# Preparing the weights at the start of a transformer kernel: biases by layout, order of the first loads, and TensorE and ScalarE in place of GpSimd

## The chip, the cores and the metric

The kernel runs on one core of a Trainium2 chip. The metric is the device time of one execution in microseconds (us). A core has five engines that each work through a queue of instructions of their own, in order: PE (TensorE, matmuls, with its weight loads), DVE (VectorE), ACT (ScalarE), POOL (GpSimd) and SP (SyncE, which here issues DMA transfers). They wait for each other by semaphores.

## What is computed

An input x of 8 sequences of 512 tokens with 256 features goes through four residual blocks: attention A, a gated feed-forward network (FFN), causal attention B, and the same FFN again.

```
x = x + attention_a(layernorm(x))
x = x + ffn(layernorm(x))
x = x + attention_b(layernorm(x))
x = x + ffn(layernorm(x))

# attention_a: 16 heads of 64; the 64 channels of one token attend to each other, causally
Q, K, V = (x @ Wq + bq) / 8, x @ Wk + bk, x @ Wv + bv        # 256 -> 1024 each
w = softmax(where(mask, -inf, Q[..., :, None] * K[..., None, :]))
out = (w @ V) @ Wo + bo
# attention_b: 16 heads of 16 over 512 tokens, causal, W_attn (256 -> 768), W_proj, biases
# ffn: silu(x W1 s1) * (x W2 s2), then gelu(. H1 h1), gelu(. H2 h2), then (. W3) s3
```

## The kernel before

Nearly all the time goes into attention A's outer products, which exist for each token and head and have no sum over a contraction that PE could do. The class `AttentionA` cuts them into steps. A tile is 128 tokens (index `i`, four to a sequence `b`) and a group of four heads (`g`, four groups); it has four units (`u`) of squares of the causal triangle, so a tile takes four steps, and the list `todo` runs over b, g, i, u. In step `n` the unit n is multiplied out (`scores`, lines 771 and 784: units 0 and 2 on POOL, 1 and 3 on DVE), unit n-1 gets its exponential on ACT (`exps`, 793 and 798), unit n-2 is weighted by V on DVE (`weigh`, 805 and 808) and, but for the smallest unit, halved by an accumulating DMA that POOL issues (`halve`, 814). Later steps fold (POOL, 819), reduce (DVE, 845) and add up the rows (POOL, 852). The projections of a tile on PE (`project`, 741 for K and 746 for Q and V) stand three steps ahead of its first unit, its normalised x eight steps ahead (`normed`, `turned_over`, 542 and 548), with the moments ten ahead (`measure`, lines 524 to 532).

The order of instructions on PE, DVE, ACT and POOL is the order in which the program writes them. Each step is written in three parts; after each part the main loop may write a piece of two other generators: `later_weights`, the preparation of weights, and `after_a`, the FFN and attention B of the sequence that has left attention A. SP's order is set by a scheduler. Blocks of SBUF of 8 KB a partition come from a pool of seven (`block`), so a late holder delays a load that wants its place.

Weights must be prepared because the normalised x carries a constant 1 in its last feature instead of the feature itself: a layer norm's features add up to zero, so that x's last feature is minus the sum of the others. The last row of a weight is therefore subtracted from every other row, and its place is taken by the bias. The steps of the beginning are, by line:

- `load_x(0)` (307) loads the first sequence, then `last_qv` and `last_k` (323, 324) are loaded as the last rows of Wq, Wv and Wk for all groups, copied to 128 partitions; then the weights of the four groups (335, 336).
- `fit_qkv(g)` subtracts the last row (344, 346; on DVE for group 0, on POOL for the others), lets SP put the bias into the last row (347, 348) and write the result to DRAM (349, 350). Group 0 is fitted before everything, groups 1 to 3 in steps 0 to 2. From then on `load_w` reads a group's weights from DRAM (624, 626).
- `later_weights` (from step 2, one piece after each part, so three a step) makes three bf16 parts of two biases with ACT, POOL and DVE (421 to 432), multiplies w3 by its scale (POOL, 451), fits attention B's weights (POOL, 456) and writes them to DRAM (460 to 462).
- It ends with `bound_scores`, which squares the weights on ACT (373, 374) after loading them again (368, 370), sums the squares in 96 small matmuls with a result of one column (382), and takes a square root (388) and maxima (389 to 402): a bound on the scores, for a flag that chooses a slower path, at the end.
- `bias_row` (468) adds a bias to a result on PE: ones in three rows times the three bf16 parts.

Of the kernel before, what the change touches and what calls it, by code (L numbers as in the profile page):

```python
# [9 lines left out]
F32 = mybir.dt.float32  # L10
F32R = mybir.dt.float32r
BF16 = mybir.dt.bfloat16
# [272 lines left out]
def fast_path(ctx: ExitStack, tc: tile.TileContext, k, t, flag):  # L285
# [24 lines left out]
    def block(name, dtype=F32):  # L310

        return hp.tile([P, HB], dtype, tag="h", name=name)

    x_first = load_x(0)

    wqv_r, wk_r = t.wqv.rearrange("(c p) g f -> p c g f", p=P), t.wqkv[1].rearrange("(c p) f -> p c f", p=P)
    wqv_d = dram.tile([NG, P, DC * 2 * GW], F32, name="wqv_d")  # L320
    wk_d = dram.tile([NG, P, DC * GW], F32, name="wk_d")
    last_qv, last_k = block("last_qv"), block("last_k")
    nc.sync.dma_start(last_qv, t.wqv[D - 1 : D].rearrange("o g f -> o (g f)").broadcast_to([P, HB]))
    nc.sync.dma_start(last_k[:, :HID], t.wqkv[1][D - 1 : D].broadcast_to([P, HID]))
    fitted = []
    for g in range(NG):
        if g == 0:

            wqv = wp.tile([P, DC, 2 * GW], F32, tag="wqv", name=f"wqv_0_{g}")
            wk = wp.tile([P, DC, GW], F32, tag="wk", name=f"wk_0_{g}")  # L330
        else:
            both = block(f"fit_{g}")
            wqv = both[:, : DC * 2 * GW].rearrange("p (c f) -> p c f", c=DC)
            wk = both[:, DC * 2 * GW : DC * 3 * GW].rearrange("p (c f) -> p c f", c=DC)
        nc.sync.dma_start(wqv, wqv_r[:, :, g, :])
        nc.sync.dma_start(wk, wk_r[:, :, g * GW : (g + 1) * GW])
        fitted.append((wqv, wk))

    def fit_qkv(g):

        wqv, wk = fitted[g]
        eng = nc.vector if g == 0 else nc.gpsimd
        qv_last = last_qv[:, g * 2 * GW : (g + 1) * 2 * GW].unsqueeze(1).to_broadcast([P, DC, 2 * GW])
        eng.tensor_tensor(wqv, wqv, qv_last, ALU.subtract)
        k_last = last_k[:, g * GW : (g + 1) * GW].unsqueeze(1).to_broadcast([P, DC, GW])
        eng.tensor_tensor(wk, wk, k_last, ALU.subtract)
        nc.sync.dma_start(wqv[P - 1 : P, DC - 1, :], t.b_qv[g : g + 1, :])
        nc.sync.dma_start(wk[P - 1 : P, DC - 1, :], t.b_a[1:2, g * GW : (g + 1) * GW])
        nc.sync.dma_start(wqv_d[g].rearrange("p (c f) -> p c f", c=DC), wqv)
        nc.sync.dma_start(wk_d[g].rearrange("p (c f) -> p c f", c=DC), wk)  # L350
# [8 lines left out]
    def bound_scores():  # L359
# [7 lines left out]
        for c in range(DC):  # L367
            nc.sync.dma_start(sqv[c], wqv_r[:, c])
        sk = block("sk").rearrange("p (c f) -> p c f", c=DC)
        nc.sync.dma_start(sk, wk_r)  # L370
        yield
        for c in range(DC):
            nc.scalar.activation(sqv[c], sqv[c], AF.Square)
            nc.scalar.activation(sk[:, c], sk[:, c], AF.Square)
            yield
# [30 lines left out]
    wbvp_d = dram.tile([P, 2 * DC * D], F32, name="wbvp_d")  # L406
    bias16 = const.tile([P, 2, D], BF16, name="bias16")[0:3]
    ones16 = const.tile([P, P], BF16, name="ones16")
    nc.gpsimd.memset(ones16, 1.0)

    def later_weights():

        braw = block("braw")[0:3].rearrange("p (n f) -> p n f", n=4)
        part16 = block("part16", BF16)[0:3, : 2 * D]
        for j, row in enumerate((t.bo, t.b_bp)):
            nc.sync.dma_start(braw[:, 0, j * D : (j + 1) * D], row.broadcast_to([3, D]))
        yield
        for j in range(3):  # L420
            nc.scalar.copy(part16, braw[:, 0])
            nc.scalar.copy(braw[:, 2], part16)
            nc.gpsimd.tensor_tensor(braw[:, 0], braw[:, 0], braw[:, 2], ALU.subtract)
            yield
            if j == 0:
                nc.vector.tensor_scalar_mul(braw[:, 3], braw[:, 2], ident[0:3, 0:1])
            else:
                nc.vector.scalar_tensor_tensor(
                    braw[:, 3], braw[:, 2], ident[0:3, j : j + 1], braw[:, 3], ALU.mult, ALU.add
                )  # L430
        yield
        nc.scalar.copy(bias16.rearrange("p j f -> p (j f)"), braw[:, 3])

# [7 lines left out]
        nc.sync.dma_start(w3, t.w3.rearrange("(c p) f -> p c f", p=P))  # L441
        nc.sync.dma_start(wbqk, t.w_bqk.rearrange("(c p) j f -> p c (j f)", p=P))
        nc.sync.dma_start(wbvp[:, 0], t.w_bv.rearrange("(c p) f -> p c f", p=P))
        nc.sync.dma_start(wbvp[:, 1], t.w_bp.rearrange("(c p) f -> p c f", p=P))
        nc.sync.dma_start(
            rows[:, :n_qk], t.w_bqk[D - 1 : D].rearrange("o j f -> o (j f)").broadcast_to([P, n_qk])
        )
        nc.sync.dma_start(rows[:, n_qk : n_qk + D], t.w_bv[D - 1 : D].broadcast_to([P, D]))
        yield
        for c in range(MC):  # L450
            nc.gpsimd.tensor_tensor(w3[:, c, :], w3[:, c, :], s3, ALU.mult)
            if c % 2:
                yield
        for w, row, cols in ((wbqk, t.b_bqk_row, slice(0, n_qk)), (wbvp[:, 0], t.b_bv, slice(n_qk, n_qk + D))):
            for c in range(DC):
                nc.gpsimd.tensor_tensor(w[:, c], w[:, c], rows[:, cols], ALU.subtract)
                yield
            nc.sync.dma_start(w[P - 1 : P, DC - 1, :], row)

# [6 lines left out]
    def bias_row(ps, j):  # L466

        nc.tensor.matmul(ps, ones16[0:3, :], bias16[:, j, :], start=False, stop=False)

# [134 lines left out]
    class AttentionA:  # L604
# [33 lines left out]
        def step(self, n):  # L638
# [16 lines left out]
            b, i, g, u = self.at(n + 10)  # L655
            if u == 0 and g == 0 and i == 0:
                self.measure(b)
# [67 lines left out]

        def measure(self, b):
            mv = small.tile([P, NT, 2], F32, tag="mv_a", name="mv", bufs=2)
            rstd = small.tile([P, NT], F32, tag="rstd_a", name="rstd", bufs=2)
            for i in range(NT):
                moments(self.x[b][:, i, :], mv[:, i, :])  # L730
            scales(mv, rstd, means[:, b, 0, :])
            for i in range(NT):
                self.rn[b, i] = rstd[:, i : i + 1], means[:, b, 0, i : i + 1]
# [607 lines left out]
    with tc.manual_schedule(engines={ET.PE, ET.DVE, ET.Activation, ET.Pool}):  # L1341
        a = AttentionA()
        prep = later_weights()
        fit_qkv(0)
        weights = None
        done, spent = after_a(), 0
        for n in range(-10, a.steps):
            for part, _ in enumerate(a.step(n)):
                if n >= 2:
                    next(prep, None)  # L1350
                while 3 * spent * each < total * (3 * (n - each - 11) + part + 1):
                    spent += next(done)
            if 0 <= n < NG - 1:
                fit_qkv(n + 1)
        for _ in done:
# [88 lines left out]
```

## Time and profile before

| | us |
|---|---|
| median of 3 runs | 4007.05 (4005.77 to 4012.08) |
| profiled execution | 4009.55 |
| its span, first to last instruction | 4007.6 |
| accumulating DMA of 1 MB (w<-w), issue to landing, median | 7.7 |
| the same in the first 160 us | 9.9 |
| matmul pass 128x512, L746, mean | 0.715 |
| matmul of the bias, L468, median of 64 | 0.278 |

The profile is taken on one execution. Its page has the busy time of each engine, then the span in 40 equal slices with each engine's busy share in tenths, the granted clock of PE (PEclk, in tenths) and the share of the 16 DMA engines; then the chain of work that ended last, and the costliest groups of instructions by line, each as output<-input. The name of an engine with a q (SPq) is its queue: there stand the issues of DMAs, which are not counted as busy. A float32 matmul is two matmul records in the trace, one for each pass.

### The profile page before, as it was taken

What the parts mean: (1) busy time and instruction counts of PE and PEld (TensorE: products, weight loads), DVE (VectorE), ACT (ScalarE), POOL (GpSimd) and SP (SyncE); (2) the same over time, 40 slices, a digit from 0 to 9 for tenths busy, and PEclk for the clock granted to TensorE, in tenths of its full rate; (3) what the DMA queues carried; (4) which work ended last, traced back from release to release, by engine and by line L of the source; (5) the groups of instructions that cost most, each with busy time, mean ns of one, the idle gap of its engine ahead of it and who ended that gap; (6) DMA issues with size and microseconds to landing.
All of it is one profiled execution on the core that took longest, in us unless ns stands there. A gap on an engine that the chain in (4) does not pass through costs nothing.

```text
span 4007.6 us, 37678 instructions
## 1 busy us (share of the span) xinstructions
PE 2958.0 (74%) x12328; PEld 2012.2 (50%) x12328; DVE 3376.7 (84%) x3777; ACT 2337.2 (58%) x3145; POOL 3098.1 (77%) x3051
## 2 busy tenths in 40 slices
PE   1543478777876888768787788768787778768988
PEld 0311145355653656346553566346653556436847
DVE  4899988998889888998989988998889988897115
ACT  2433465666755766666755767567656667555342
POOL 6688888887888887887888888888888878886211
PEclk7555689888987989889897889879898899879999
DMA  8566777668776777668776688668877687767304
GB/s 240 114 141 145 146 182 182 147 161 199 199 162 126 195 188 196 150 147 210 174 192 139 168 198 214 147 131 198 195 181 151 154 199 205 155 133 210 126 29 167
DMA packets 118653, 671.07 MB, mean 167 GB/s; under 512 B 12704, under 2 KB 31915, under 8 KB 43824
## 3 DMA queue, kind: packets, MB, share of 16 engines
q0 software_dynamic: 78336, 570.46, 62.9%
q1 hardware_dynamic: 40112, 98.11, 6.8%
q8 instruction: 100, 1.64, 0.2%
q14 instruction: 105, 0.86, 0.1%
HBM read 255.90 MB, written 9.96 MB: 66 GB/s over the span
## 4 chain that ended last, share of the span: by engine, by line
DVE 38%; PE 16%; POOL 14%; DMA 12%; issue 8%; ACT 8%; POOLq 0%; DVEq 0%; ACTq 0%
DVE red L845 15%; DMA w<-w 12%; DVE w L808 10%; PE ph L1120 5%; ACT w L798 3%; POOL w L819 3%; DVE ws L808 3%; POOL w L784 3%; PE pqkb L1167 3%; DVE ws L784 3%; POOL acc L852 3%; DVE w L784 2%; POOL w L814 2%; DVE acc L856 2%; POOL h L1036 2%
## 5 line engine op out<-in xcount | busy, mean ns | idle before, releaser
L798 ACT ACTIVATE w<-w 128x2048 f32<-128x2048 f32 x384 | 734.2, 1913 | 653.8 <-POOL w L784 440.8
L1120 PE MATMUL ph<-h,hidden 128*128 128x512 f32 x4096 | 1047.9, 412 | 77.4 <-POOL h L1036 45.5
L784 POOL TENSOR_TENSOR w<-k 128x1024 f32<-128x1024 f32 x512 | 1076.2, 2102 | 9.6 <-ACT k L762 9.0
L1120 PEld LDWEIGHTS ph<-h,hidden 128*128 128x128 f32 x4096 | 795.3, 196 | 282.1 <-POOL h L1036 55.9
L808 DVE TENSOR_TENSOR w<-w,qv 128x1024 f32<-128x1024 f32 x768 | 899.8, 1213 | 22.4 <-ACT w L798 22.3
L845 DVE TENSOR_REDUCE red<-w 128x128 f32<-128x1024 f32 (+1 forms) x384 | 601.8, 1567 | 171.6 <-DMA w<-w 94.6
L819 POOL TENSOR_TENSOR w<-w 128x1024 f32<-128x1024 f32 x256 | 643.1, 2512 | 72.5 <-DMA w<-w 71.9
L814 POOL DMA_DIRECT2D w<-w x384 | 337.1, 878 | 339.7 <-issue 134.8
L852 POOL TENSOR_TENSOR acc<-acc,red 128x256 f32<-128x256 f32 (+1 forms) x640 | 471.0, 736 | 152.3 <-DVE red L845 124.5
L845 DVE TENSOR_REDUCE red<-ws 128x256 f32<-128x2048 f32 (+1 forms) x256 | 435.5, 1743 | 0.0
L746 PE MATMUL qv<-wqv,xnta 128*128 128x512 f32 x512 | 299.3, 715 | 89.9 <-DVE ws L808 82.4
L808 DVE TENSOR_TENSOR ws<-ws,qv 128x1024 f32<-128x1024 f32 (+3 forms) x512 | 294.7, 638 | 49.4 <-ACT ws L798 49.4
L1052 PE MATMUL pw<-xnt,gate 128*128 128x512 f32 (+2 forms) x1152 | 298.8, 419 | 24.9 <-ACT silu L1028 18.0
L784 DVE TENSOR_TENSOR w<-qv,k 128x1024 f32<-128x1024 f32 x256 | 301.3, 1219 | 3.6
L784 DVE TENSOR_TENSOR ws<-qv,k 128x1024 f32<-128x1024 f32 (+3 forms) x512 | 299.8, 648 | 0.0
L868 PE MATMUL bank<-ident,acc 128*128 128x128 f32 x256 | 64.3, 341 | 287.5 <-ACT k L761 287.1
L798 ACT ACTIVATE ws<-ws 128x1920 f32<-128x1920 f32 x128 | 231.5, 1809 | 75.3 <-DVE ws L784 74.7
L1052 PEld LDWEIGHTS pw<-xnt,gate 128*128 128x128 f32 x1152 | 227.6, 213 | 82.1 <-ACT silu L1028 22.3
L1229 ACT ACTIVATE eb<-psb 128x256 f32<-128x256 f32 (+3 forms) x512 | 182.2, 443 | 146.6 <-PE psb L1226 146.3
L1146 PE MATMUL pof<-w,h 128*128 128x256 f32 x1024 | 247.9, 396 | 19.4 <-ACT h L1085 19.4
L1085 ACT ACTIVATE h<-ph,s_sb 128x512 fp32r<-128x512 f32 (+1 forms) x256 | 171.1, 688 | 145.9 <-PE ph L1120 144.6
L856 DVE RECIPROCAL acc<-acc 128x256 f32<-128x256 f32 x128 | 223.2, 1744 | 12.3 <-POOL acc L852 12.3
(143 smaller groups left out, 4723.5 us busy)
## 6 DMA issues: line engine op xcount, KB each, us to landing
w<-w POOLq DMA_DIRECT2D x384, 1024.0 KB, 7.7
hidden<-in_h POOLq DMA_DIRECT2D x128, 1024.0 KB, 7.9
gate<-in_w12p POOLq DMA_DIRECT2D x32, 1024.0 KB, 9.0
w<-w_d SPq DMA_DIRECT2D x16, 1024.0 KB, 12.0
wqv<-wqv_d SPq DMA_DIRECT2D x31, 512.0 KB
wo<-in_wo SPq DMA_DIRECT2D x32, 256.0 KB, 7.4
wbqk<-wbqk_d SPq DMA_DIRECT2D x8, 1024.0 KB
w<-in_h SPq DMA_DIRECT2D x8, 1024.0 KB, 7.0
```

Of the source, the lines that this page charges most:

```text
L746: nc.tensor.matmul(qv.rearrange("p j f -> p (j f)"), xnt[:, c, :], wqv[:, c, :], start=(c == 0), stop=(c == DC - 1),)
L784: eng.tensor_tensor(e, rows(q).to_broadcast(shape), columns(kt[:, 0]).to_broadcast(shape), ALU.mult)
L798: nc.scalar.activation(e, e, AF.Exp, scale=C**-0.5)
L808: nc.vector.tensor_tensor(ev, e, columns(qv[:, 1]).to_broadcast(list(e.shape)), ALU.mult)
L814: nc.gpsimd.dma_start(w[:, :2048], w[:, 2048:], accum_op=ALU.add)
L819: nc.gpsimd.tensor_tensor(w[:, :1024], w[:, :1024], w[:, 1024:2048], ALU.add)
L845: nc.vector.tensor_reduce(red, self.columns_of(w, n, off, nsq), AX.X, ALU.add)
L852: nc.gpsimd.tensor_tensor(rows, rows, part.rearrange("p a (x i) -> p a x i", i=n), ALU.add)
L856: nc.vector.reciprocal(acc[:, 0, :], acc[:, 0, :])
L1052: nc.tensor.matmul(pj[:, toks], w[:, m % 4, j, c, :], xs[:, p, c, toks], start=(p == 0 and c == 0), stop=(p == 1 and c == DC - 1),)
L1120: nc.tensor.matmul(pss[j], w[:, j, c, :], h_in(p, c), start=(p == 0 and c == 0), stop=(p == 1 and c == MC - 1),)
L1146: nc.tensor.matmul(po, h(0, c)[:, i * P : (i + 1) * P], w3[:, c, :], start=(c == 0), stop=False)
```

## The change

The bias now lies in the last row of the weight from the start (arrays `wqvb`, `wkb`, `w_bqkb`, `w_bvb`, laid out before the launch), and the subtraction leaves that row out. The DMAs that put a bias in place are gone. The original rows are still read from `wqv` and `wqkv`.

The first loads are the first tile of x, the weights of group 0 and their last rows for this group alone; the other tiles of x, the other groups and the last rows as single rows follow. `measure` takes a range of tiles: the first tile's moments are taken before group 0 is fitted, those of the other three after it. `fit_first` subtracts in four DVE instructions, two of them over 127 partitions.

The other groups and attention B's weights are fitted by `less_row`: an identity matmul brings a part of the weight to PSUM, a matmul of one row (-1 for every row but the last, times the last row) subtracts from it, and ACT copies the result back one step later. w3 is scaled two chunks at a time. `later_weights` now starts at step 3 and writes one piece a step; it takes in the groups 1 to 3, then w3, attention B and the bounds. The two biases stay float32, one row each, in `rows_of_1`.

```diff
+    x_first = xp.tile([P, NT, D], F32, tag="x", name="x_0")
+    nc.sync.dma_start(x_first[:, 0, :], t.x[0, :P, :])
...
-    last_qv, last_k = block("last_qv"), block("last_k")
-    nc.sync.dma_start(last_qv, t.wqv[D - 1 : D].rearrange("o g f -> o (g f)").broadcast_to([P, HB]))
-    nc.sync.dma_start(last_k[:, :HID], t.wqkv[1][D - 1 : D].broadcast_to([P, HID]))
+    last_first = block("last_first")
...
         nc.sync.dma_start(wqv, wqv_r[:, :, g, :])
         nc.sync.dma_start(wk, wk_r[:, :, g * GW : (g + 1) * GW])
+        if g == 0:
+            row_qv, row_k = last_first[:, : 2 * GW], last_first[:, 2 * GW : 3 * GW]
+            nc.sync.dma_start(row_qv, t.wqv[D - 1 : D, 0].broadcast_to([P, 2 * GW]))
+            nc.sync.dma_start(row_k, t.wqkv[1][D - 1 : D, :GW].broadcast_to([P, GW]))
+            for i in range(1, NT):
+                nc.sync.dma_start(x_first[:, i, :], t.x[0, i * P : (i + 1) * P, :])
...
+    def fit_first():
+
+        wqv, wk = fitted[0]
+        for w, row in ((wqv, row_qv), (wk, row_k)):
+            for c, rows in enumerate((slice(0, P), slice(0, P - 1))):
+                nc.vector.tensor_tensor(w[rows, c], w[rows, c], row[rows], ALU.subtract)
...
+    def less_row(w, c, row, p0):
+
+        ps = ps_f.tile([P, 2 * GW], F32, tag="pf", name="pfit")[:, : w.shape[-1]]
+        nc.tensor.matmul(ps, ident, w, start=True, stop=False)
+        nc.tensor.matmul(ps, from_rows[p0 : p0 + 1, c, :], row, start=False, stop=True)
+        return ps
+
     def fit_qkv(g):
...
-        eng.tensor_tensor(wqv, wqv, qv_last, ALU.subtract)
...
-        eng.tensor_tensor(wk, wk, k_last, ALU.subtract)
-        nc.sync.dma_start(wqv[P - 1 : P, DC - 1, :], t.b_qv[g : g + 1, :])
-        nc.sync.dma_start(wk[P - 1 : P, DC - 1, :], t.b_a[1:2, g * GW : (g + 1) * GW])
...
+        for w, row, p0 in rows:
+            pss = [less_row(w[:, c], c, row, p0) for c in range(DC)]
+            yield
+            for c, ps in enumerate(pss):
+                nc.scalar.copy(w[:, c], ps)
+            yield
...
             nc.scalar.activation(sqv[c], sqv[c], AF.Square)
+            yield
             nc.scalar.activation(sk[:, c], sk[:, c], AF.Square)
...
-        for j in range(3):
-            nc.scalar.copy(part16, braw[:, 0])
-            nc.scalar.copy(braw[:, 2], part16)
-            nc.gpsimd.tensor_tensor(braw[:, 0], braw[:, 0], braw[:, 2], ALU.subtract)
...
+            nc.sync.dma_start(biases[j][:, :D], row)
+        for g in range(1, NG):
+            yield from fit_qkv(g)
...
-        for c in range(MC):
-            nc.gpsimd.tensor_tensor(w3[:, c, :], w3[:, c, :], s3, ALU.mult)
-            if c % 2:
-                yield
...
-                nc.gpsimd.tensor_tensor(w[:, c], w[:, c], rows[:, cols], ALU.subtract)
-                yield
-            nc.sync.dma_start(w[P - 1 : P, DC - 1, :], row)
+        for c in range(0, MC, 2):
+            pair = w3[:, c : c + 2, :]
+            nc.gpsimd.tensor_tensor(pair, pair, s3.unsqueeze(1).to_broadcast(list(pair.shape)), ALU.mult)
+            yield
+        for w, off, width in ((wbqk, 0, 2 * GW), (wbqk, 2 * GW, 2 * GW), (wbvp[:, 0], 0, D)):
+            row = rows[0:1, n_qk if width == D else off :][:, :width]
+            pss = [less_row(w[:, c, off : off + width], c, row, 0) for c in range(DC)]
+            yield
+            for c, ps in enumerate(pss):
+                nc.scalar.copy(w[:, c, off : off + width], ps)
+            yield
...
-        nc.tensor.matmul(ps, ones16[0:3, :], bias16[:, j, :], start=False, stop=False)
+        nc.tensor.matmul(ps, biases[j][:, D:], biases[j][:, :D], start=False, stop=False)
...
-        fit_qkv(0)
+        a.measure(0, range(1))
+        fit_first()
+        a.measure(0, range(1, NT))
...
-                if n >= 2:
+                if n >= 3 and part == 2:
                     next(prep, None)
...
-            if 0 <= n < NG - 1:
-                fit_qkv(n + 1)
```

## The prediction

> **What bounds the kernel now.** I read the page first (busy shares, the 40 slices), then the windows of the beginning, the chain of waits, the list of waits and the timeline of the first 165 us.
>
> ```profile
> PE 2958.0 (74%) x12328; PEld 2012.2 (50%) x12328; DVE 3376.7 (84%) x3777; ACT 2337.2 (58%) x3145; POOL 3098.1 (77%) x3051
> ...
> DVE  4899988998889888998989988998889988897115
> ...
> 27.91:53.21 25.30, 3.98 (x12) 1.93 (x12) 15.01 (x18) 12.96 (x17) 23.79 (x15) 0.68 0.52 140
> 53.21:85.78 32.57, 5.08 (x10) 2.62 (x10) 22.44 (x25) 9.30 (x9) 31.54 (x30) 0.55 0.98 291
> 85.78:141.08 55.30, 26.56 (x115) 22.16 (x115) 26.45 (x32) 16.64 (x15) 23.13 (x20) 0.56 0.57 140
> 141.08:164.87 23.79, 9.83 (x18) 4.38 (x18) 23.76 (x26) 9.64 (x11) 19.98 (x18) 0.57 0.55 112
> 164.87:188.59 23.72, 9.68 (x18) 4.20 (x18) 23.68 (x26) 9.12 (x9) 20.74 (x19) 0.64 0.66 133
> ```
>
> The second line is DVE's busy tenths in slices of 100 us: full until the last tenth, except the first slice. The windows (columns: length, busy us of PE, PE weight load, DVE, ACT, POOL, then clock, DMA share, GB/s) run from one tile's first score (DVE, L771) to the next. From 141 us on, a tile takes 23.72 us with DVE busy for 23.68 of them: DVE sets the pace. The three tiles before took 25.30, 32.57 and 55.30 us, and DVE worked for only 63.9 of those 113.2.
>
> ```profile
> 12.91 1.23 DVE L344 TENSOR_TENSOR wqv<-wqv,last_qv 128x1024 f32<-128x1024 f32 x1 [10.39 <-DMA wqv<-in_wqv]
> ...
> 22.44 2.07 PE L741 MATMUL bank<-wk,xnta 128*128 128x256 f32 x4 [0.46 <-ACT xnta L669]
> ...
> 27.91 0.42 DVE L771 TENSOR_TENSOR acc<-qv,k 128x256 f32<-128x256 f32 x1 [11.03 <-ACT k L762]
> ...
> 31.78 2.35 POOL L344 TENSOR_TENSOR fit<-fit,last_qv 128x1024 f32<-128x1024 f32 x1
> ...
> 87.34 1.40 SPq L370 DMA_DIRECT2D sk<-in_wqkv  x1
> ...
> 107.15 1.06 ACT L374 ACTIVATE sk<-sk 128x1024 f32<-128x1024 f32 x1 [21.88 <-DMA sk<-in_wqkv]
> ...
> 110.86 1.79 ACT L798 ACTIVATE ws<-ws 128x1920 f32<-128x1920 f32 x1
> ...
> 112.68 2.35 DVE L808 TENSOR_TENSOR ws<-ws,qv 128x1024 f32<-128x1024 f32 x4 [24.68 <-ACT ws L798]
> ...
> 141.08 0.41 DVE L771 TENSOR_TENSOR acc<-qv,k 128x256 f32<-128x256 f32 x1
> ```
>
> The timeline (start, us, instruction; in brackets the idle time before it and what ended it) names the losses: DVE waits to 12.91 for weights; the first score comes at 27.91; POOL does weights between scores; and at 85 us ACT stands in its own order before the Square of sk, whose load SP issued only at 87.34. That load costs DVE 24.68 us. Then PE works through the norms (L382, in the chain from 110.06 to 129.82) with the projections of the fourth tile among them.
>
> **What the skill says.** The Trainium skill, "SBUF — State Buffer", section "Who interferes with whom", says a VectorE instruction with two SBUF inputs contends with a GpSimd instruction that reads SBUF. The trace fits: L390, 24 elements a partition, took 1.38 us beside POOL. So weight work taken from POOL also frees DVE a little; I count nothing for it. The same page, "The DMA setup-cost knee", gives about 2 us fixed for a transfer; the x loads of 128 KB here land in 2.0 us (median). "TensorE: Matmul & The Clock Gate", "What's actually happening", says an idle TensorE runs at half clock; PEclk is 0.5 in 100 to 125 us. I price new matmuls at the slow durations. "ScalarE: Activation LUTs", "What ACT_TABLE_LOAD costs", says 1283 ns; the trace has 1.28 us at L388.
>
> **The change part by part.**
>
> First weights. Before, x (0.5 MB), two broadcast blocks (1.5 MB) and wqv (0.5 MB) stood ahead of the first subtraction: 2.5 MB at 153, 303 and 307 GB/s in the first three windows of 4 us. Now one x tile, wqv, wk and two short rows are needed: 0.13 + 0.5 + 0.25 + 0.26 + 0.13 = 1.27 MB, reached at about 6.1 us by those rates; with 2 us of landing, 8.3 us (bounds 7 and 10). Four subtractions 512, 512, 256, 256 wide: 512 took 0.69 on DVE, 256 about 0.42: 2.2 us. Three tiles' moments at 0.53: 1.6. POOL's scales 2.0, ACT xn 0.65, PE transposes 0.7, ACT copy 0.4: the first L741 at about 16.0 instead of 22.44. The first tile's xn is made earlier now, so only one xn is in that chain. From L741 to L771 it stays 5.5 us. First score at 21.6 instead of 27.91: 6.3 us. The two one-row DMAs of the bias into wqv and wk (L347, L348), which SP had issued after DVE, go too.
>
> The first three tiles. POOL loses three pairs of L344 and L346 (3 x 2.35 + 4.4 = 11.5), three L423 (4.3), L456 twice 2.34 and twice 0.96 (6.6). What remains, walked through with the durations above: POOL's first scores 21.6 to 25.4, ACT exp to 27.3, DVE L808 to 29.7, w16 to 32.1, ws to 34.4, second scores back from ACT at 35.0, DVE to 37.4, so the second tile's L771 at 37.8. The next period has stalls of about 2 us for the accumulating DMA (8 us from issue) and ends at 62.5. The third is steady: 86.2. DVE's own work from first to fourth L771 was 63.9 - 2.9 (L426, L428, gone) - 2.8 (norm, moved) = 58.2; my 64.6 is that with 6.4 of stalls. Against 141.08: **54.9 us** less.
>
> What comes after 86 us that was before 141:
> - Three groups' weights on PE and ACT (L365, L366, L380 of the new file). A 128x512 float32 matmul is two passes of 0.94 at half clock (3.75 for four); a wqv part is eight passes, 7.5 us, a wk part 4.2. A period has 9.4 busy on PE: 21.1 of 23.7 with both. They stand behind a projection (done about 6 us after DVE's L808 of ws) and ahead of nothing due within a step; the ACT copies (0.6 + 0.6 for 512 wide, as L1188's 599 ns) come one step of 5.93 us later, ACT being busy 9.1 of 23.7 and idle about 3 before each exp. I take 0; without the cover 9 copies times 2 us = 18.
> - SP: the write-backs wait for ACT, and the reload of group 1 (L643) stands behind one of them (L382 of group 2). That copy is done a step earlier than PE frees wqv, so 0.
> - w3 (L469): four POOL products 512 wide, L346's 1.27 to 1.71 each, 5.6 us in one period in which POOL waits 2.7 for DVE (before L814). Cost 0 to 5.6: I take 3.
> - Norms: DVE about 2.8, ACT 2 x 1.28 + 0.19 for the table. The pn matmuls are now six a step, not 18. The Squares' loads are issued long before (their buffers come free near 75 to 97 us, they are used near 180), so ACT doesn't stand before them. 2 to 5: 3.
> - Traffic: sqv, sk and the write-backs, some 5 MB, fall beside accumulating DMAs of a steady loop whose DMA share is 0.66. L845 has about a microsecond to spare (halving issued 232.05, reduced 240.14, 7.7 us median landing; the first 160 us had 9.9). Two DMAs a period, 2.2 us each, in one or two periods: 0 to 10, I take 5.
> - bias_row: 0.278 us in bf16 with 0.43 of idle before it (27.6 over 64) against two float32 passes of 0.28 to 0.5. Only 4 of 64 lie in the PE-bound last 400 us: within 1 us of nothing. I take 0.
>
> Sum: 54.9 - 3 - 3 - 5 = 43.9. The profiled execution took 4009.55 (span 4007.6), 2.5 over the median 4007.05; the gain is taken off the median: **3963 us**. All later work is paced by DVE from the same order, so the shift reaches the end whole.
>
> **Rivals.**
> 1. A wait replaces the waits: loads collide with the accumulating DMAs, and POOL's w3, each at its upper bound and lasting three periods rather than one: 13 + 6 + 5 = 24, and the first tiles take another 10. Gain 21, 3986 us. For it: the share of 0.98 between 53 and 86 us. Against: 2.1 MB of broadcasts are gone, and most loads are issued before the first accumulation.
> 2. Everything hides: 54.9 less the 2 us of norm work on DVE, 3954 or, with first weights a microsecond sooner and less lock contention, down to 3945. Against: POOL has only 2.7 us to spare in a period.
> 3. Slower: in each of the 39 steps that now carry a part of the preparation (24 of weights, 15 of norms), ACT stands in its own order before a copy until PE's slow float32 matmuls end, and the exp behind it comes late for DVE. It decides from 54.9 / 39 = 1.4 us a step. At 1.8 us: 4007 - 55 + 70 = 4022. For it: exactly this order cost 24.7 us at sk. Against: one step lies between each matmul and its copy, and PE has room.
> 4. No effect: the beginning is filled but a later wait (PE in the FFN's order) takes it up: 4007. DVE's 84% against PE's 74%, with PE bound only in the tail, speaks against it.
>
> **How the numbers follow.** Forecast 0.60 (own range 3952 to 3976), rival 1 0.20, rival 2 0.12, rival 3 0.05, rival 4 0.03. The range 3946 to 3987 takes the forecast, most of rival 2 and half of rival 1: about 0.8. A measurement here can tell 0.2%, 8 us. Faster: 0.60 + 0.12 + nearly all of rival 1; same: rival 4 and an edge of rival 1; slower: rival 3.
>
> **What would show it.** In the profile after: the first L791 (old L771) near 21.6, the next near 38, 62 and 86; DVE's first slice at 7 tenths, not 4; no wait of 20 us before any Square; steady periods of 23.7 with 3 to 8 us lost near the w3 products, the sqv loads and the norm. Wrong would be: ACT waiting for PE before L380 by more than a microsecond each, periods of 26 us through the preparation, or a first score later than 25.

## The result

The kernel after takes 3989.26 us (median of 4 runs, 3985.6 to 3992.53) against 4009.57 us for the kernel before on the same chip (4 runs): a ratio of 0.9949, 95% interval 0.9931 to 0.9966. It is faster by 20 us where the prediction had 44, and 2 us outside the predicted range, 3946 to 3987.

The page of the kernel after, its busy times and DVE's tenths in slices of 100 us:

```profile
PE 3039.9 (76%) x12464; PEld 2055.2 (52%) x12464; DVE 3375.9 (85%) x3776; ACT 2341.3 (59%) x3156; POOL 3077.9 (77%) x3040
...
DVE  7999988998899888998899988998989888996115
```

DVE's first slice went from 4 to 7, as foreseen. PE is 81.9 us busier than before. The timeline of the beginning (start, us, instruction, idle time before it), and then the windows from one tile's first score (DVE, L791, the old L771) to the next (length, busy us of PE, PE weight load, DVE, ACT and POOL, clock, DMA share, GB/s):

```profile
7.79 1.29 DVE L357 TENSOR_TENSOR wqv<-wqv,last_first 128x512 f32<-128x512 f32 x2 [4.21 <-DMA last_first<-in_wqv]
...
15.09 2.07 PE L761 MATMUL bank<-wk,xnta 128*128 128x256 f32 x4 [0.46 <-ACT xnta L688]
...
20.29 0.42 DVE L791 TENSOR_TENSOR acc<-qv,k 128x256 f32<-128x256 f32 x1 [8.93 <-ACT k L782]
```

```profile
20.29:36.53 16.24, 7.99 (x20) 3.19 (x20) 12.16 (x15) 9.61 (x11) 11.74 (x7) 0.78 0.70 199
36.53:62.91 26.38, 13.81 (x28) 6.08 (x28) 22.25 (x24) 10.32 (x13) 19.26 (x17) 0.63 0.97 228
62.91:86.67 23.76, 17.72 (x30) 7.15 (x30) 23.73 (x25) 10.28 (x14) 20.82 (x19) 0.57 0.83 211
86.67:113.36 26.69, 13.52 (x27) 6.22 (x26) 23.87 (x26) 10.62 (x13) 20.87 (x19) 0.56 0.88 226
113.36:138.95 25.59, 17.83 (x26) 6.98 (x26) 23.77 (x26) 9.12 (x9) 24.48 (x22) 0.57 0.70 144
...
260.88:290.07 29.19, 10.70 (x22) 5.77 (x23) 28.95 (x32) 11.88 (x12) 21.79 (x19) 0.62 0.66 144
290.07:313.78 23.71, 7.87 (x14) 3.29 (x13) 23.68 (x25) 9.12 (x9) 19.93 (x18) 0.64 0.61 123
```

The first four tiles start at 20.29, 36.53, 62.91 and 86.67 us; 21.6, 37.8, 62.5 and 86.2 were predicted. The fourth is 54.4 us earlier than before (predicted 54.9). So the beginning was right; what is missing was lost later.

**Where the lead goes.** I call "lead" how much earlier a tile's first score comes than the same tile's in the kernel before; there are 128 tiles, 0 to 127, sixteen to a sequence. In the kernel after the lead is 54.4 us at tile 3, 40.8 at tile 11, the same 40.8 at tile 18, and then only 34.3 at tile 64, 26.9 at tile 96 and 20.7 at tile 127. From tile 127 to the end another 3.9 are lost (372.6 against 368.7 us), which leaves the difference of the two spans, 4007.6 - 3990.8 = 16.8. The shift did not reach the end whole: half of it went in the steady loop, where by the prediction nothing of the change was left.

To find the place, I took each interval from one tile's first score to the next, less the same interval before, and added these up over tiles 32 to 127 (six sequences) by the tile's position in its sequence. Two positions carry 12.2 us: position 2 loses 6.6 and position 13 loses 5.6. Each of the twelve intervals is longer than before, position 13's by 0.8 to 1.0 us every time; no other position comes above 3.1. At position 2 the timeline shows the following, first in the kernel before, then in the kernel after, from the first bias of attention A in a sequence:

```profile
2372.78 0.39 PE L468 MATMUL bank<-bias,ones 3*128 3x256 bf16 x1
...
2373.10 1.22 PE L472 MATMUL bank<-x,ident 128*128 128x256 f32 x2
...
2374.12 1.06 PE L548 MATMUL ps_ln<-ident,xn 128*128 128x128 f32 x4
...
2375.19 0.85 DVE L983 TENSOR_TENSOR xnt<-ps_ln,xnt 128x256 fp32r<-128x256 f32 x2 [1.65 <-ACT xnt L976]
```

```profile
2342.31 1.22 PE L487 MATMUL bank<-rows_of 1*128 1x256 f32 x2
...
2343.45 1.22 PE L491 MATMUL bank<-x,ident 128*128 128x256 f32 x2
...
2344.47 1.06 PE L567 MATMUL ps_ln<-ident,xn 128*128 128x128 f32 x4
...
2345.55 0.85 DVE L1003 TENSOR_TENSOR xnt<-ps_ln,xnt 128x256 fp32r<-128x256 f32 x2 [2.50 <-ACT xnt L996]
```

From the bias to the next matmul PE takes 0.32 us with three bf16 rows (2372.78 to 2373.10) and 1.14 with one float32 row (2342.31 to 2343.45): 0.82 longer. The transposes of a layer norm stand behind it on PE, ACT casts them, and DVE, in order, waits 2.50 us instead of 1.65: 0.85 longer. The granted clock of PE is 0.50 in both stretches. So it is at both positions in all six sequences: PE takes 1.14 or 1.15 us for the first bias, against 0.32 before. The next bias of the same sequence, at 2374.63, where the granted clock is 1.00, takes 0.62 against 0.21, and position 3, where it falls, loses nothing (-0.1). Position 13 is the same thing with attention B's first bias (before, then after):

```profile
1271.19 0.39 PE L468 MATMUL pob<-bias,ones 3*128 3x256 bf16 x1
...
1271.51 1.22 PE L472 MATMUL pob<-x,ident 128*128 128x256 f32 x2
...
1272.53 0.71 PE L1292 MATMUL pytb<-ident,ytb 128*128 128x128 f32 x4
...
1273.49 0.25 DVE L1260 RECIPROCAL yb<-pytb 128x16 f32<-128x16 f32 x1
```

```profile
1233.95 1.22 PE L487 MATMUL pob<-rows_of 1*128 1x256 f32 x2
...
1235.10 1.22 PE L491 MATMUL pob<-x,ident 128*128 128x256 f32 x2
...
1236.12 1.06 PE L1312 MATMUL pytb<-ident,ytb 128*128 128x128 f32 x4
...
1237.22 0.26 DVE L1280 RECIPROCAL yb<-pytb 128x16 f32<-128x16 f32 x1 [0.89 <-PE pytb L1312]
```

Before, the reciprocal followed without a wait; after, it waits 0.89 us for PE. In all six sequences this wait is 0.88 or 0.89 us, where it was 0.00 to 0.06. `bias_row` is the one edit of this change that runs in every sequence to the end, and the prediction had taken it at nothing.

### The profile page after: what moved, and what is told of

Read it like the earlier page. It is cut to its first block, busy times and chain, and to the rows that moved or that the text cites. A ratio compares the mean times of both kernels' runs of the same rounds, so it can differ in the third digit from the quotient of the medians.

```text
span 3990.8 us, 37932 instructions
## 1 busy us (share of the span) xinstructions
PE 3039.9 (76%) x12464; PEld 2055.2 (52%) x12464; DVE 3375.9 (85%) x3776; ACT 2341.3 (59%) x3156; POOL 3077.9 (77%) x3040
## 3 DMA queue, kind: packets, MB, share of 16 engines
q8 instruction: 101, 1.65, 0.2%
## 4 chain that ended last, share of the span: by engine, by line
DVE 38%; PE 18%; POOL 14%; DMA 13%; ACT 8%; issue 8%; SPq 0%; ACTq 0%; POOLq 0%; DVEq 0%
DVE red L865 15%; DMA w<-w 13%; DVE w L828 10%; PE ph L1140 5%; ACT w L818 4%; POOL w L804 3%; POOL w L839 3%; DVE ws L828 3%; PE pqkb L1187 3%; POOL acc L872 3%; DVE w L804 2%; DVE ws L804 2%; POOL h L1056 2%; POOL w L834 2%; DVE acc L876 2%
## 5 line engine op out<-in xcount | busy, mean ns | idle before, releaser
L804 POOL TENSOR_TENSOR w<-k 128x1024 f32<-128x1024 f32 x512 | 1077.4, 2104 | 7.7 <-ACT k L782 7.1
L839 POOL TENSOR_TENSOR w<-w 128x1024 f32<-128x1024 f32 x256 | 643.7, 2514 | 82.9 <-DMA w<-w 82.3
L828 DVE TENSOR_TENSOR ws<-ws,qv 128x1024 f32<-128x1024 f32 (+3 forms) x512 | 294.3, 635 | 27.6 <-ACT ws L818 27.6
L804 DVE TENSOR_TENSOR w<-qv,k 128x1024 f32<-128x1024 f32 x256 | 301.1, 1218 | 3.6
L804 DVE TENSOR_TENSOR ws<-qv,k 128x1024 f32<-128x1024 f32 (+3 forms) x512 | 299.5, 646 | 0.2 <-issue 0.2
```

What stands on the lines that cost most here:

```text
L804: eng.tensor_tensor(e, rows(q).to_broadcast(shape), columns(kt[:, 0]).to_broadcast(shape), ALU.mult)
L828: nc.vector.tensor_tensor(ev, e, columns(qv[:, 1]).to_broadcast(list(e.shape)), ALU.mult)
L839: nc.gpsimd.tensor_tensor(w[:, :1024], w[:, :1024], w[:, 1024:2048], ALU.add)
```

## The experiments

Theory R: the float32 rows of `bias_row` cost DVE about 1 us at two places of each sequence, because PE's granted clock is 0.50 there and DVE's next instruction hangs on PE. Its rivals: that the preparation's traffic or the place of buffers in SBUF slows the loop (placement), or that the loop simply scatters. All kernels were run beside the kernel before, whose medians were 4009 to 4012 us.

**Three bf16 rows in the kernel after.** The rows are zeros and the parts are not made, so both biases' values and their two loads are left out, and later buffers lie at other offsets; all else is the kernel after.

```diff
-        nc.tensor.matmul(ps, biases[j][:, D:], biases[j][:, :D], start=False, stop=False)
+        nc.tensor.matmul(ps, ones16[0:3, :], bias16[:, j, :], start=False, stop=False)
```

> The changed kernel with bias_row as before: three bf16 rows against ones. It leaves out the values of the two biases (the rows are zeros) and the work of making the parts, so it shows the form of the matmul alone. Theory R (the float32 row lengthens PE's chain at every sequence; the last score came 20 us nearer to before than the eighteenth, and the span 4 more): about 3989 - 22 = 3967 us, the last score 40 us ahead of before as at the eighteenth tile, about 3598. Rival S (the loss is one of phase: A's steps meet the FFN's orders and transfers differently, whatever form the bias has): 3987 to 3991, the last score at 3616 to 3620.

3969.16 us, ratio 0.9903 (0.9887 to 0.9919). The lead is 40.1 at tile 18 and 42.5 at tile 127; positions 2 and 13 lose 1.8 and -0.5 us instead of 6.6 and 5.6. It takes 20 us less than the kernel after. The two positions account for 10.9 us in the traces; the rest is taken up below.

**One float32 row in the kernel before.** The new form without the rest of the change. Two small loads bring the rows, and the bf16 parts are still made, but not used:

```diff
-        nc.tensor.matmul(ps, ones16[0:3, :], bias16[:, j, :], start=False, stop=False)
+        nc.tensor.matmul(ps, biases[j][1], biases[j][0], start=False, stop=False)
```

> The kernel before with bias_row as after: one float32 row against ones at partitions 64 and 96, loaded by two small DMAs more; the bf16 parts are still made but not used. R: about 4008 + 22 = 4030 us, the first 18 tiles as before within 1 us, and the tiles where the changed kernel lost (those that carry attention B's end and attention A's first group) about 1 us longer each. S: 4008 within 3.

4023.46 us, ratio 1.0035 (1.0023 to 1.0047). Less than R's figure, but the form costs the kernel before 14 us as well: with it the run is 3.4 us ahead of the kernel before at tile 18 and 8.7 behind at tile 127, with 5.1 us lost at position 2 and 5.1 at position 13.

**No bias at all.** Both calls of `bias_row` are left out of the kernel after, so that PE has less to do than with bf16 rows.

```diff
-            if g == 0:
-                bias_row(po, 0)
...
-            bias_row(po, 1)
```

> The changed kernel without any bias_row matmul (both biases are left out). It bounds what a cheaper form can give. R: 3960 to 3966, some 4 to 8 us below the one with bf16 rows, because a bf16 row costs PE 0.28 us and a gap against about 1.2 us and two gaps. S: 3985 to 3991.

3981.89 us, ratio 0.9922 (0.9906 to 0.9938), not the 3960 to 3966 that R expected. Positions 2 and 13 lose nothing (-0.4, -0.6), as R has it, and yet the lead falls from 40.2 to 27.6. It goes at other places, position 1 above all (+4.2, where the bf16 rows have -4.4). There DVE waits for an accumulating DMA; the same reduction without biases and then with three bf16 rows:

```profile
2286.88 2.29 DVE L865 TENSOR_REDUCE red<-w 128x256 f32<-128x2048 f32 x1 [2.53 <-DMA w<-w]
```

```profile
2280.36 2.29 DVE L865 TENSOR_REDUCE red<-w 128x256 f32<-128x2048 f32 x1 [0.66 <-DMA w<-w]
```

So there is scatter of some 10 us beside R, and not only between kernels: the six runs of this one reach from 3971.14 to 3985.82, and the lowest lie among those of the kernel with three bf16 rows (3966.11 to 3975.12). It had to be told from R, and placement, too: this kernel and the kernel after had their later buffers at other offsets than the one with three bf16 rows.

**Placement alone.** The float32 rows stay; an unused constant tile moves the later buffers to the offsets of the fast kernel.

```diff
+    spare = const.tile([P, 192], F32, name="spare")
+    nc.gpsimd.memset(spare[:, :1], 0.0)
```

> The kernel after, with 0.75 KB per partition of an unused constant tile, so that all later SBUF buffers lie at the same offsets (modulo 1 KB) as in e1_bf16_rows; the float32 rows stay. Theory R (the float32 one-row matmul costs DVE its lead at the attentions' projections): as the kernel after, 3985 to 3992 us; the lead over the kernel before is about 41 at tile 18 and about 21 at the last tile, and tile positions 2 and 13 modulo 16 lose 5 us each over tiles 32 to 127. Rival A (placement: the buffers' addresses decide, and e1's were luckier): about 3969 us, with a lead that stays at 40.

3990.34 us, ratio 0.9946 (0.9932 to 0.9959), and the lead falls from 39.5 to 20.9, with 7.2 and 5.9 at the two positions: the kernel after again. These offsets are not what made the other kernel fast.

**One of the two rows.** Attention A's bias as bf16 rows of zeros, attention B's as it is.

```diff
-        nc.tensor.matmul(ps, biases[j][:, D:], biases[j][:, :D], start=False, stop=False)
+        if j == 0:
+            nc.tensor.matmul(ps, ones16[0:3, :], bias16[0:3, :], start=False, stop=False)
+        else:
+            nc.tensor.matmul(ps, biases[j][:, D:], biases[j][:, :D], start=False, stop=False)
```

> The kernel after, with attention A's bias as bf16 rows of zeros (its values are left out) and attention B's row in float32 as it is. Theory R: only attention B's place (tile position 13) loses, 5 to 6 us over tiles 32 to 127, position 2 loses under 2, and the tail's extra 4 us stay: 3976 to 3982 us. Rival A (placement): no connection between position and which row is float32; both or neither lose.

3982.96 us, ratio 0.9924 (0.9911 to 0.9938). Position 2 loses 0.5, position 13 still 5.5: each position belongs to its row.

**One bf16 row at the same partitions.** It parts the number of rows and their place from the data type.

```diff
-        nc.tensor.matmul(ps, biases[j][:, D:], biases[j][:, :D], start=False, stop=False)
+        nc.tensor.matmul(ps, ones16[64 + 32 * j : 65 + 32 * j, :], bias16[64 + 32 * j : 65 + 32 * j], start=False, stop=False)
```

> The kernel after, with each bias as one bf16 row of zeros at partitions 64 and 96 (values left out): the same one-row form and place as the kernel after, in one pass. If the two float32 passes and their weight loads are the cost: as e1_bf16_rows, 3966 to 3972 us, lead flat at 40. If a matmul of one row at a high partition is the cost: as the kernel after, 3985 to 3992 us.

3970.28 us, ratio 0.9906 (0.9893 to 0.992), positions 2 and 13 at 0.3 and -0.2. The timeline at position 2 is that of the kernel before:

```profile
2335.09 0.39 PE L489 MATMUL bank<-bias,ones 1*128 1x256 bf16 x1
...
2335.41 1.22 PE L493 MATMUL bank<-x,ident 128*128 128x256 f32 x2
...
2337.50 0.85 DVE L1005 TENSOR_TENSOR xnt<-ps_ln,xnt 128x256 fp32r<-128x256 f32 x2 [1.63 <-ACT xnt L998]
```

It is the data type, not the single row. The lines of the two forms, three bf16 rows before and one float32 row after (min/median/max in ns, first and last start, forms), show what it consists of:

```profile
L468 PEld LDWEIGHTS <-ones x64: 90/91/99, 134.6 to 3899.8; 3*128 3x128 bf16 x64
...
L468 PE MATMUL pob<-bias,ones x32: 277/278/389, 810.1 to 3899.8; 3*128 3x256 bf16 x32
```

```profile
L487 PEld LDWEIGHTS pob<-rows_of x64: 181/184/333, 770.1 to 3883.4; 1*128 1x128 f32 x64
L487 PE MATMUL pob<-rows_of x64: 374/478/792, 770.1 to 3883.6; 1*128 1x256 f32 x64
```

A float32 row needs two weight loads of 184 ns and two passes of 478 ns (medians; 64 records for 32 calls), a bf16 row one of 91 and one of 278. A pass here is one matmul record of the trace; whether PE runs through just once for it is not shown. For the weight loads this agrees with the Trainium skill, "TensorE: Matmul & The Clock Gate", section "Weight-path perf modes — Fast Weight Load (FWL) and DoubleRow": the fast load is on for 128 weights that are not FP32. That this mode was on here is not seen in the trace, only the 91 and 184 ns.

**The suspected cost doubled.** A second float32 row, with weights of zeros, ahead of each bias.

```diff
+        p = 64 + 32 * j
+        nc.tensor.matmul(ps, zeros[p : p + 1], biases[j][:, :D], start=False, stop=False)
         nc.tensor.matmul(ps, biases[j][:, D:], biases[j][:, :D], start=False, stop=False)
```

> The kernel after, with a second float32 one-row matmul (weights of zeros) ahead of each bias row: the suspected cost doubled. Theory R: the cost repeats. Tile positions 2 and 13 lose 11 to 14 us each over tiles 32 to 127, twice what the kernel after loses; the lead of about 41 at tile 18 is down to 0 to 5 at the last tile; the tail loses another 4: 4008 to 4018 us, no faster than the kernel before (4009 to 4012). Rival C (the loss is scatter of the steady loop and not the rows' time): about as the kernel after, 3985 to 3995.

3997.22 us, ratio 0.9962 (0.9949 to 0.9976). Positions 2 and 13 lose 10.5 and 11.0, against 6.6 and 5.6: the cost there nearly doubles. At position 13 the reciprocal waits 1.73 or 1.74 us in all six sequences. The time rose by 8 us and not by the 19 to 29 expected, because only these two positions doubled; the expectation was written as if all that the lead loses were R's. At position 2:

```profile
2347.21 1.22 PE L490 MATMUL bank<-rows_of,zeros 1*128 1x256 f32 x2
2348.23 1.05 PE L491 MATMUL bank<-rows_of 1*128 1x256 f32 x2
2349.21 1.22 PE L495 MATMUL bank<-x,ident 128*128 128x256 f32 x2
```

```profile
2351.30 0.85 DVE L1007 TENSOR_TENSOR xnt<-ps_ln,xnt 128x256 fp32r<-128x256 f32 x2 [3.32 <-ACT xnt L1000]
```

DVE's wait here is 1.65 with bf16 rows, 2.50 with one float32 row and 3.32 with two.

**The norms.** `bound_scores`, its loads with it, is left out of the kernel after and its two results are set to zero.

```diff
-        yield from bound_scores()
+        nc.vector.memset(over[0:1, 0:2], 0.0)
```

> The kernel after without the norms of the score bound (bound_scores is left out and its two results are set to zero). The prediction put them at 3 us; the trace of the kernel after has one period of 29.2 instead of 23.7 beside them. If the norms own that period: the lead at tile 11 is 46 instead of 40.8, the difference stays to the end, 3983 to 3986 us. If something else (write-backs, w3) falls due there: lead 41 to 43, 3987 to 3990.

3977.56 us, ratio 0.9917 (0.9903 to 0.993). The lead at tile 11 is 49.3 instead of 40.8, 8.5 more; 1.3 of it is there at the first score already, and 5.5 is the period at 260.88, which is 23.72 us without the norms and 29.19 with them; the other 1.7 are gained between tiles 3 and 7, with the loads of sqv and sk gone. The time fell by 11.7 us, more than the expected 3 to 6: on the way to the last tile this kernel also loses less than the kernel after, which cannot be put down to the norms. DVE is busy through the period at 260.88, so this is no wait. The timeline shows what the norm's two small instructions do beside POOL; first the kernel before, where POOL stood idle from 127.77 to 130.58 and worked on a product from 133.50 to 135.46, then the kernel after, first POOL, then DVE:

```profile
129.96 0.17 DVE L389 SCALAR_TENSOR_TENSOR babs<-babs 128x24 f32<-128x24 f32 x1
134.11 1.38 DVE L390 TENSOR_TENSOR norm<-norm,babs 128x24 f32<-128x24 f32 x1 [3.98 <-ACT norm L388]
```

```profile
270.56 2.35 POOL L839 TENSOR_TENSOR w<-w 128x1024 f32<-128x1024 f32 x1
272.87 1.95 POOL L804 TENSOR_TENSOR w<-k 128x1024 f32<-128x1024 f32 x1
```

```profile
270.77 2.18 DVE L423 SCALAR_TENSOR_TENSOR babs<-babs 128x24 f32<-128x24 f32 x1
273.06 1.80 DVE L424 TENSOR_TENSOR norm<-norm,babs 128x24 f32<-128x24 f32 x1
```

L423 begins 0.21 us after POOL's L839 and ends at 272.95, just after POOL's end at 272.91; L424 ends at 274.86, POOL's L804 at 274.82. Two instructions on 24 elements a partition took about as long as POOL's on 1024. The kernel with one bf16 row gives the other side. There POOL's fold is held up by an accumulating DMA, and the same two instructions fall into the pause:

```profile
272.68 0.17 DVE L423 SCALAR_TENSOR_TENSOR babs<-babs 128x24 f32<-128x24 f32 x1
272.95 0.18 DVE L424 TENSOR_TENSOR norm<-norm,babs 128x24 f32<-128x24 f32 x1
...
273.90 2.37 POOL L841 TENSOR_TENSOR w<-w 128x1024 f32<-128x1024 f32 x1 [1.37 <-DMA w<-w]
```

Its period took 26.02 us: 2.3 for the norms instead of 5.5. In the ten other kernels that have the norms in the steady loop, the kernel after among them, the period took 29.2.

**The scales of w3.** POOL's products are left out of the kernel after; w3 stays unscaled.

```diff
-            nc.gpsimd.tensor_tensor(pair, pair, s3.unsqueeze(1).to_broadcast(list(pair.shape)), ALU.mult)
             yield
```

> The kernel after with w3's products with its scales on GpSimd left out (w3 stays unscaled). The prediction put them at 3 us. If they own what the tiles 4 to 7 lose (54.4 to 46.2 of lead) beside the transfers: the lead at tile 7 is 49 to 50 and stays 3 to 4 higher to the last tile, 3984 to 3987 us. If the transfers of sqv and sk own it: lead at tile 7 46 to 47, 3988 to 3990 us.

3989.38 us, ratio 0.9946 (0.9933 to 0.996): no gain in the time, and a lead at tile 7 of 47.3, between the two expectations. From tile 4 to tile 7, where the products stand, this kernel loses 2.3 us of lead; the kernel after loses 5.2 there, and its other variants with the products 4.9 to 6.6. But the edit moves transfers as well. With no product to wait for, SP issues the write-back of w3 at 41.61 us instead of 139.27, and the first load of sqv at 61.84 instead of 77.89. This run has then lost 4.8 already before tile 3: DVE waits 1.79 us for an accumulating DMA and 3.55 for POOL's fold, which had itself waited 4.16 for one. The kernel after has neither wait there. From tile 3 to 4 this run loses nothing (the kernel after 3.0), and its lead at tile 18 is only 1 higher, 41.8. So it doesn't part the products from the transfers.

**Three complete versions with bf16 rows.** All make the biases' three parts again. The first loads the biases where the old code did and makes two parts before the first score:

```diff
+    bias_steps = {
+        -5: lambda: (bias_part(), bias_place(0)),
+        -3: lambda: (bias_part(), bias_place(1)),
+        1: bias_part,
+        3: lambda: bias_place(2),
+    }
```

> The changed kernel with bf16 rows whose parts are made from the biases as before, in the stretch before the first score in which ACT, POOL and DVE stand idle (steps -5, -3, 1 and 3). R: as the one with zero rows plus what the parts delay the first score, 0 to 3 us: 3967 to 3971, better than both. S: 3989 to 3994.

3983.68 us, ratio 0.9933 (0.9918 to 0.9949). The lead is 32.9 at tile 18 and 33.3 at tile 127: flat, but 8 lower from the start. ACT stood in its order before a bias load that SP had issued at 13.13 us, and the first score came at 25.57:

```profile
15.90 0.62 ACT L453 CAST part<-braw 3x512 bf16<-3x512 f32 x1 [9.05 <-DMA braw<-in_b_bp]
```

The second issues these loads directly behind the first group's and makes two parts before the first score.

```diff
+            for j, row in enumerate((t.bo, t.b_bp)):
+                nc.sync.dma_start(braw[:, 0, j * D : (j + 1) * D], row.broadcast_to([3, D]))
             for i in range(1, NT):
...
+        bias_part(0)
+        bias_part(1)
```

> The kernel after, complete, with the biases as three bf16 rows (as before), whose loads stand directly behind the first group's rows and whose parts are made before and between the first steps. Theory R: e1_bf16_rows plus 0 to 3 us for the parts: 3968 to 3973 us, faster than both the kernel before (4009) and after (3989), lead flat near 40. Rival A: somewhere from 3969 to 3989 by chance of placement. If the bias preparation delays the first score as in e4_bf16_real (25.57 us): 3980 to 3984 us.

3980.25 us, ratio 0.9919 (0.9906 to 0.9933). The first score comes at 23.82, the lead is 33.1 at tile 18 and falls to 25.2 with 0.8 lost at positions 2 and 13 together: scatter again. The third makes the parts after the first score, with two instructions that subtract a part only in the partitions that do not hold it:

```diff
+    def bias_part(j):
+        nc.scalar.copy(part16, braw[:, j])
+        nc.vector.scalar_tensor_tensor(braw[:, j + 1], part16, keep_part[j], braw[:, j], ALU.mult, ALU.subtract)
+
+    bias_steps = {
+        1: lambda: bias_part(0),
+        3: lambda: bias_part(1),
+        5: lambda: nc.scalar.copy(bias16.rearrange("p j f -> p (j f)"), braw[:, 2]),
+    }
```

> The kernel after, complete, with the biases as three bf16 rows, made by three casts on ScalarE and two small subtractions on VectorE in steps 1, 3 and 5, after the first score. Theory R: the first score stays at 20 to 21 us, the first tiles lose at most 3, the lead at tile 18 is 37 to 41 and flat to the last tile: 3967 to 3974 us, the fastest complete version. If e9_bf16_early_bias was slow for another reason than its late first score: about 3980.

3977.82 us, ratio 0.9918 (0.9905 to 0.9932); its five runs, 3972.76 to 3982.15, lie below all runs of the kernel after. The timeline has its first score in time:

```profile
19.74 0.42 DVE L811 TENSOR_TENSOR acc<-qv,k 128x256 f32<-128x256 f32 x1 [8.59 <-ACT k L802]
```

Tile 3 is 2.8 us later than in the kernel after, the lead at tile 18 is 37.5 and at tile 127 38.8: flat. The median is 4 us above the expected range. It computes everything and is faster than both kernels.

**All runs side by side.** Worked out from the traces, one profiled execution of each kernel: the lead at tiles 18 and 127, what positions 2 and 13 lose over tiles 32 to 127, and the rest of what the lead loses from 18 to 127.

| kernel | median us | lead at 18 | lead at 127 | pos. 2 | pos. 13 | rest |
|---|---|---|---|---|---|---|
| after | 3989.26 | 40.8 | 20.7 | 6.6 | 5.6 | 7.9 |
| spare tile | 3990.34 | 39.5 | 20.9 | 7.2 | 5.9 | 5.5 |
| no w3 products | 3989.38 | 41.8 | 24.1 | 6.6 | 5.7 | 5.5 |
| no norms | 3977.56 | 49.3 | 38.3 | 4.7 | 5.8 | 0.6 |
| before, float32 rows | 4023.46 | 3.4 | -8.7 | 5.1 | 5.1 | 1.8 |
| float32 rows twice | 3997.22 | 41.6 | 12.5 | 10.5 | 11.0 | 7.7 |
| attention A bf16 | 3982.96 | 40.4 | 30.6 | 0.5 | 5.5 | 3.8 |
| three bf16 rows | 3969.16 | 40.1 | 42.5 | 1.8 | -0.5 | -3.8 |
| one bf16 row | 3970.28 | 42.1 | 40.0 | 0.3 | -0.2 | 2.0 |
| no rows | 3981.89 | 40.2 | 27.6 | -0.4 | -0.6 | 13.6 |
| complete, loads as before | 3983.68 | 32.9 | 33.3 | -0.0 | 0.0 | -0.4 |
| complete, loads early | 3980.25 | 33.1 | 25.2 | 0.8 | 0.0 | 7.1 |
| complete, parts late | 3977.82 | 37.5 | 38.8 | -0.7 | 0.1 | -0.7 |

The two columns of positions follow the edit in every row; the last column, -4 to 14 us, follows none that I can name, and it may change from one execution of a kernel to the next. The kernels with bf16 rows carry the same preparation and, but for one, keep their lead, so the preparation is not what slows the later loop.

## Why the prediction was wrong

**Right: the first tiles.** The first L761 at 15.09 (predicted 16.0), the four starts within 1.4 us of the walk-through, 54.4 us for 54.9. One reading was off without harm: the 2.0 us for the landing of an x load is that of one load early in the trace, and the median over the whole run is 7.0.

**Right: weights on PE and ACT, and SP's order, at nothing.** ACT's copies L380 and L476 waited for PE 0.3 us in all, so rival 3's premise, ACT standing before PE in each step, is not seen. Rival 4, in which a later wait for PE takes up the whole gain, did not come true, since 20 us remain. But it was the only one to look for the loss in later waits for PE; the wait came from the change's own rows and not from the FFN's order.

**Too small: the norms.** 3 us were taken (2 to 5), with DVE's 2.8 from the kernel before; they cost 5.5. The term left the same instructions their old durations, although the prediction itself had cited why L390 took 1.38 us: the Trainium skill, "SBUF — State Buffer", "Who interferes with whom", where DVE with two SBUF inputs contends with POOL's reads. L423 has two SBUF inputs as well; it had taken 0.17 with POOL idle. In a period in which POOL works 20 of 24 us it was likely to meet POOL, and only one of eleven traces shows it in a pause.

**Right in the sum, by luck: w3 and the traffic.** 3 + 5 were taken. The lead fell 54.4 - 40.8 = 13.6 by tile 18; less 5.5 for the norms that is 8.1, lost between tiles 3 and 7. In these four periods DVE waits five times, 7.7 us in all. Four of the waits, 6.8 us, lead to an accumulating DMA, two of them by way of a fold of POOL that waited for it. The fifth, 0.88 at 152.40, is for a fold that POOL, at work without a pause since the products, reached late. In the products' own period DVE's only wait was over before the first product began:

```profile
119.41 2.29 DVE L865 TENSOR_REDUCE red<-w 128x256 f32<-128x2048 f32 x1 [1.78 <-DMA w<-w]
...
119.80 1.52 POOL L469 TENSOR_TENSOR w<-w,rows 128x512 f32<-128x512 f32 x1
```

By these waits about 7 us belong to late accumulating DMAs and about 1 to the products. That the loads of sqv and sk delay these DMAs is seen beside the run without the norms, which doesn't have them: of the accumulating DMAs issued from 75 to 115 us, five of six land within 7.3 us there, and none in less than 9.9 in the kernel after. But that run still loses 6.4 between tiles 3 and 7, and which other transfers this comes from was not tested.

**The step that failed** is the last of the part by part list: bias_row, with "Only 4 of 64 lie in the PE-bound last 400 us: within 1 us of nothing. I take 0", and with it "All later work is paced by DVE from the same order, so the shift reaches the end whole." The durations were about right: two passes of 0.28 to 0.5 were priced, the median is 0.478, and until the next matmul the row took 0.62 or 1.14 us. Wrong was the cover. That DVE paces the loop on average does not say that PE has slack everywhere: twice in a sequence DVE's next instruction hangs on PE within microseconds of a bias, and there PE, at its slow passes, takes 0.82 us longer for it. Over six sequences that is 12.2 us.

The account, in the two profiled executions: 43.9 predicted, less 3.1 by tile 18, less 12.2 at the two positions, less 7.9 elsewhere between tiles 18 and 127, less 3.9 in the tail, leaves 16.8. Shown are the 12.2 (rows off in two ways, one of the two off alone, both doubled) and 2.5 of the 3.1, by which the norms exceeded their term. Not settled are the 7.9 and the 3.9. As to the 7.9, the table shows that the loop scatters by as much with no edit to blame; the kernel without rows shows it at the accumulating DMAs, but why their landing shifts was not found. The tail took 370.9 to 375.3 us in the kernels with a float32 row and 367.9 to 371.9 in those with bf16 rows only, the kernel before among them; doubling did not lengthen it (370.9), so I leave it open whether it belongs to R. The four biases in it take PE 0.62 us each instead of 0.21, so that 1.6 of the 3.9 could be theirs.

Rival 1 (3986 us) was nearest in time, but by chance: the first tiles did not take another 10, the late DMAs took about 7, not 13, and it had nothing for the bias rows.

## What to carry to other kernels

An edit that runs in every iteration deserves a place-by-place look even if its engine is not the bound: find each instance, see what stands behind it on its engine and who waits for that, before it is costed at nothing. A lead gained at the start is worth following tile by tile to the end; differences summed by position in the loop name the place within one pair of traces. And a tiny VectorE instruction with two SBUF inputs, moved into a loop in which GpSimd seldom rests, may have to be priced at GpSimd's instruction: here at 2.18 us, not at 0.17.

## What the runs showed of the hardware

- A one-row float32 matmul of 128x256 kept PE 1.14 us until its next matmul where the granted clock was 0.50, and 0.62 where it was 1.00 (1246.64 to 1247.26 us), against 0.32 and 0.21 in bf16. One or three bf16 rows made no difference (median 278 ns for both).
- DVE instructions with 24 elements a partition took 2.18 and 1.80 us and ended within 0.05 us of POOL's of 1024; in a pause of POOL the same two took 0.17 and 0.18.
- Taking work away from PE (no bias at all) gave 3981.89 us where a bf16 row gave 3970.28, with runs that overlap (3971.14 to 3985.82 and 3968.64 to 3983.62). In the two traces the loop's accumulating DMAs land differently, and DVE waits for them elsewhere. A few us of one kernel prove little here without the place.
